# Layer 0 of a four-layer graph network: the transposed adjacency by turning bytes on chip instead of a second load, with an earlier first load and a first product across six PSUM banks

## The chip, the core and the metric

The kernel runs on one core of a Trainium2 chip, as one launch. Its inputs lie in the chip's memory, and the host only lays them out (it also writes a transposed copy of the adjacency, `adjt`). The metric is the device time of one execution in microseconds (us); the time before is the median of three runs.

A core has five engines that run side by side, each with its own queue of instructions in a fixed order: TensorE (PE, matrix products; PEld is its loading of the stationary operand), VectorE (DVE), ScalarE (ACT), GpSimd (POOL) and SyncE (SP, which here only issues transfers). Sixteen DMA engines move data between the memory and the core's SBUF. Products land in PSUM, which has eight banks of 2 KiB per partition; one partition is one of 128 rows.

## The reference

There are 16 samples of 1024 nodes with 128 features, and an adjacency `adj` of 1024 x 1024 int32 per sample, zeros and ones. Four graph layers follow each other, each with a residual and a layer norm; layers 1 to 3 are attention layers and are not touched here. Layer 0, cut to what matters:

```python
adjT = transpose(adj.astype(float32), (0, 2, 1))
w = masked_row_softmax(adjT)          # adj is 0/1: every neighbour gets 1/count
region = matmul(w, features)
region = batch_norm(matmul(region, kernel_1) + bias_1)
people = matmul(transpose(w, (0, 2, 1)), region)
people = batch_norm(matmul(people, kernel_2) + bias_2)
x = layernorm(x + people)
```

The batch norms take their means and squares over all samples, so all 16 samples must pass both products with the adjacency before layer 0 has an output.

## The kernel before

`fast_path` holds everything (a slower general path runs only where a flag says that `adj` was not of zeros and ones, which ACT finds out by summing squares). Layer 0 is the block from L657 to L799. It uses that the products with the small kernels commute with those over the graph: per sample it makes `zr`, the sum of the neighbours' features with a count; `zf`, `zr` over the count; `zw`, `zf` over the count again; and `yf`, the sum of `zw` over the transposed adjacency. What the batch norms need is gathered over all samples as two Gram matrices (`gram`, L674), of `zf` and of `yf`, each summed in a PSUM bank of its own. `yf` is stored to the memory as `people`, from where the later layers read it.

The products run in bf16 with float32 sums. `split3` (L721) cuts a float32 tile into three bf16 parts, whose sum is the value: ACT casts, DVE subtracts, ACT casts the rest, DVE subtracts again. The parts stand side by side as 3 x 130 = 390 columns, in `xs` (of x; the column behind the first part is one, and gives the count) and `zs` (of `zw`). The adjacency is the stationary operand: an int32 of zero or one, whose lowest byte is read as an 8-bit float with a stride of four bytes.

`product` (L737) runs over eight chunks c of 128 nodes. For each it takes one of six PSUM banks (`f_pz`), makes eight matmuls of 390 columns (L744), and lets DVE add the three parts in one reduce from 387 to 129 columns (L747), which frees the bank.

`region(b)` (L757) loads the sample's `adj` as four tiles of 1 MiB (`f_at`, six slots; `load_adj`, L729), loads and splits x of the next sample (`features`), has ACT do the eight sums of squares (L765), multiplies, and has DVE do the count, its reciprocal, `zf` (L774), `zw` (L775) and the split of `zw`. `spread(b)` (L779) loads the sample's `adjt` as four more tiles of 1 MiB (`f_att`, six slots), multiplies with `zs`, stores `yf` on ACT's queue (L786) and adds to a Gram matrix. The loop (L793) calls region of sample b and then spread of sample b − 1, so that PE has a product to make while DVE and ACT prepare the next moving operand:

```python
for b in range(B + 1):
    now = region(b) if b < B else None
    if yf is not None:
        gram(1, yf, b - 2)
    yf = spread(b - 1, *held) if b else None
    held = now
```

Each engine's order in layer 0 is set by the framework's scheduler from this program; where a buffer has slots, a load waits until the last reader of its slot is done. In front of the loop, six small loads of the weights stand first in SP's queue (L576 to L587), and PE makes a few products of weights alone (L637 to L647: three transposes into one bank, copies by ACT, three narrow products into another). They are used by `first_norm` in the last sample and in the layers behind. After layer 0, a short stretch computes the second batch norm, and layers 1 to 3 run from a plan with a fixed order that is written out in the file; it reads `adjt` itself and is not touched.

## Time and profile before

| | |
|---|---|
| median of three runs | 1693.37 us (1692.27 to 1694.13) |
| the profiled execution's own time | 1691.56 us |
| its span (first to last instruction) | 1689.7 us |
| mean granted clock of TensorE | 0.981 |
| layer 0, to its last product | 0 to 421.4 us |
| PE busy over the span | 1608.6 us (95%) |
| DVE, ACT, POOL busy | 1306.2 (77%), 1122.9 (66%), 361.2 us (21%) |
| read from the memory, written | 377.89 MB, 16.91 MB |

Some conventions of the views below. A row of the stage windows gives a stretch in us, its length, the busy time of PE, PEld, DVE, ACT and POOL with the number of instructions, the clock granted to TensorE, the mean busy share of the 16 DMA engines, and GB/s. A row of groups gives line, engine and operation, the output and inputs by name with their shapes, how many, then busy us and mean ns of one, then the engine's idle time ahead of them and what ended it. A row of a timeline gives the start in us, the duration, the engine and the instructions (x9: nine in a row), and in brackets the wait ahead of it and what ended it. SPq is SP's queue, where a DMA is issued. Matmuls are pipelined: the mean of one contains overlap with its neighbours.

The stretch around 240 to 265 us serves as the steady sample: one passage of the loop, with region of one sample and spread of the one before. Over layer 0 the period of the loop is 25.27 us.

### The profile page before, as it was taken

The numbers are of one execution on the slowest core, as the hardware profiler recorded it, in microseconds if no ns is written. First come the engines' busy times: TensorE is split into PE (matmuls) and PEld (weight loads), VectorE is DVE, ScalarE is ACT, GpSimd is POOL, SyncE is SP. The second block draws the span as 40 slices with busy tenths as digits, with TensorE's granted clock in tenths as the row PEclk, the third lists the DMA queues.
The fourth block names the chain that finished last, engine by engine and source line by source line (L and its number), as shares of the span: only waits on it lengthen the run. The fifth ranks groups of instructions, "written<-read, shape, count | busy, mean of one in ns | idle before, by whom it ended". The sixth has DMA issues, their size and how long they took to land. (4 is left out here: it accounts for less than half of the span.)

```text
span 1689.7 us, 34809 instructions
## 1 busy us (share of the span) xinstructions
PE 1608.6 (95%) x13007; PEld 1443.5 (85%) x13023; DVE 1306.2 (77%) x2924; ACT 1122.9 (66%) x2911; POOL 361.2 (21%) x615
## 2 busy tenths in 40 slices
PE   6999999999569999999999999999999999999996
PEld 4666666666468999999999999999999999999996
DVE  4565565565367889898988989898898989898775
ACT  6555555552446777778677777877777787777575
POOL 0000000000121232323233132422323241331221
PEclk9999999999579999999999999999999999999999
DMA  8999999997355667667766666777666676766652
GB/s 319 382 365 393 362 372 392 352 388 280 115 184 175 200 183 213 201 203 215 214 205 200 205 196 210 215 210 206 210 194 194 217 210 205 211 189 195 187 158 77
DMA packets 395155, 397.16 MB, mean 235 GB/s; under 512 B 11104, under 2 KB 339680, under 8 KB 394976
## 3 DMA queue, kind: packets, MB, share of 16 engines
q1 hardware_dynamic: 378336, 386.45, 70.3%
q10 hardware_dynamic: 16640, 8.39, 1.7%
q8 instruction: 104, 1.70, 0.4%
q14 instruction: 75, 0.61, 0.1%
HBM read 377.89 MB, written 16.91 MB: 234 GB/s over the span
## 5 line engine op out<-in xcount | busy, mean ns | idle before, releaser
L1191 PE MATMUL f_pbank<-f_rows,f_p 128*128 128x129 f32 x4096 | 495.6, 275 | 0.8 <-DVE f_p L1178 0.8
L1191 PEld LDWEIGHTS f_pbank<-f_rows,f_p 128*128 128x128 f32 x4096 | 475.2, 191 | 3.6 <-DVE f_q L1045 2.6
L1141 PE MATMUL f_pbig<-f_xt,f_hw 128*128 128x128 f32 x2304 | 303.1, 276 | 3.9 <-ACT f_xt L977 1.5
L1141 PEld LDWEIGHTS f_pbig<-f_xt,f_hw 128*128 128x128 f32 x2304 | 279.0, 192 | 7.2 <-ACT f_xt L977 1.8
L1170 DVE TENSOR_TENSOR f_q<-f_q,f_e 128x1024 f32<-128x1024 f32 (+7 forms) x256 | 193.5, 756 | 117.1 <-ACT f_q L1163 88.8
L1163 ACT ACTIVATE f_q<-f_pbig,f_neg_shift 128x1024 f32<-128x1024 f32 (+7 forms) x256 | 189.3, 739 | 140.7 <-PE f_pbig L1155 139.2
L1091 PE MATMUL f_pbig<-f_q,f_p 128*128 128x128 f32 x2048 | 254.4, 278 | 5.7 <-ACT f_q L1085 5.7
L1091 PEld LDWEIGHTS f_pbig<-f_q,f_p 128*128 128x128 f32 x2048 | 242.7, 194 | 7.1 <-ACT f_q L1085 7.1
L1167 ACT ACTIVATE f_e<-f_pbig,f_neg_shift 128x1024 f32<-128x1024 f32 (+7 forms) x256 | 188.4, 736 | 37.2 <-PE f_pbig L1155 32.0
L1178 DVE TENSOR_TENSOR f_p<-f_q,f_a 128x1024 f32<-128x1024 f32 (+7 forms) x256 | 192.5, 752 | 1.9
L744 PE MATMUL f_pz<-f_zs,f_att 128*128 128x390 bf16 x1024 | 181.0, 328 | 3.1 <-DVE f_yf L747 2.9
L744 PE MATMUL f_pz<-f_xs,f_at 128*128 128x390 bf16 x1024 | 178.9, 330 | 4.9 <-DVE f_xs L727 4.2
L765 ACT ACTIVATE f_junk<-f_at,f_sq_bias 128x1024 bf16<-128x1024 int32 x128 | 146.9, 1148 | 51.4 <-DVE f_yf L747 47.9
L1076 DVE SCALAR_TENSOR_TENSOR f_p<-f_u,f_r,f_u 128x1024 f32<-128x1024 f32 x128 | 163.3, 1276 | 6.4 <-DMA f_u<-f_u_dram 6.4
L744 PEld LDWEIGHTS <-f_at 128*128 128x128 fp8e4 x1024 | 100.1, 98 | 73.0 <-issue 6.1
L744 PEld LDWEIGHTS <-f_att 128*128 128x128 fp8e4 x1024 | 100.1, 98 | 69.6 <-issue 6.5
L1079 DVE SCALAR_TENSOR_TENSOR f_p<-f_p,f_a 128x1024 f32<-128x1024 f32 x128 | 156.3, 1221 | 2.3
L1182 DVE TENSOR_TENSOR f_p<-f_pbig,f_a 128x128 f32<-128x128 f32 (+6 forms) x224 | 152.4, 680 | 0.1
L747 DVE TENSOR_REDUCE f_zr<-f_pz 128x129 f32<-128x387 f32 x128 | 63.2, 552 | 111.8 <-PE f_pz L744 111.7
L952 POOL TENSOR_SCALAR f_ln_var<-f_sq 128x1 f32<-128x1 f32 (+2 forms) x96 | 38.5, 401 | 500.3 <-ACT f_junk L941 500.3
L1155 PE MATMUL f_pbig<-f_ident,f_q 128*128 128x128 f32 x896 | 135.1, 273 | 4.1 <-DVE f_q L1170 3.4
L914 ACT ACTIVATE f_junk<-f_rows,f_total 128x128 f32<-128x128 f32 x256 | 102.7, 401 | 15.2 <-DVE f_rows L1015 5.1
(160 smaller groups left out, 2121.5 us busy)
## 6 DMA issues: line engine op xcount, KB each, us to landing
f_a<-in_adjt_dram SPq DMA_DIRECT2D x384, 512.0 KB, 4.5
f_at<-in_adj_dram SPq DMA_DIRECT2D x64, 1024.0 KB, 9.3
f_att<-in_adjt_dram SPq DMA_DIRECT2D x64, 1024.0 KB, 13.7
f_u<-f_u_dram SPq DMA_DIRECT2D x32, 512.0 KB, 5.8
f_xn<-in_x_dram SPq DMA_DIRECT2D x16, 512.0 KB, 11.2
f_people<-f_yf ACTq DMA_DIRECT2D x16, 512.0 KB, 16.9
f_yn<-f_people SPq DMA_DIRECT2D x16, 512.0 KB, 3.8
f_x<-in_x_dram SPq DMA_DIRECT2D x16, 512.0 KB, 4.4
```

Source lines behind the costliest of these rows:

```text
L744: nc.tensor.matmul(pz[:, :3 * K], a8[:, j % 2, c * 512:(c + 1) * 512:4], moving[:, j].rearrange("p k d -> p (k d)"), start=(j == 0), stop= ...
L765: nc.scalar.activation(junk, at[c // 2][:, c % 2, :], AF.Square, bias=sq_bias, accum_out=squares[:, b, c:c + 1])
L1076: p = op(DVE, 1.2, lambda e, t, t2, *_, j=j: nc.vector.scalar_tensor_tensor(e, t2, ln.r[:, j:j + 1], t, ALU.mult, ALU.max), [key("r", j)], ...
L1079: op(DVE, 1.24, lambda t, e, j=j: nc.vector.scalar_tensor_tensor(e, e, 1.0, t.rearrange("p c n -> p (c n)"), ALU.mult, ALU.mult, accum_out ...
L1091: nc.tensor.matmul(t[:, c * D:(c + 1) * D], q[:, c * P:(c + 1) * P], hn[:, j, :], start=False, stop=(j == C - 1 and c % 4 == 3))
L1141: nc.tensor.matmul(t[:, j * P:(j + 1) * P], hw[:, j * P:(j + 1) * P], xt[:, mine], start=True, stop=True)
L1163: nc.scalar.activation(q[:, blocks, :], t[:, c * P:].rearrange("p (c n) -> p c n", n=P), AF.Exp, bias=neg_shift)
L1167: nc.scalar.activation(e[:, c * P:], t[:, c * P:], AF.Exp, bias=neg_shift, scale=SLOPE)
L1170: nc.vector.tensor_max(q[:, blocks, :], q[:, blocks, :], e[:, c * P:].rearrange("p (c n) -> p c n", n=P))
L1178: nc.vector.tensor_mul(t[:, c * P:].rearrange("p (c n) -> p c n", n=P), q[:, blocks, :], k[:, c:, :])
L1182: nc.vector.tensor_mul(t[:, :c * P].rearrange("p (c n) -> p c n", n=P), s[:, :c * P].rearrange("p (c n) -> p c n", n=P), k[:, :c, :])
L1191: nc.tensor.matmul(t[:, :D + 1], w[:, j * P:(j + 1) * P], xl[:, j, :], start=(j == 0), stop=(j == C - 1))
```

## The change

Only layer 0 and what stands in front of it change.

- The loads of x and adj of sample 0 are issued first, then the six weight loads (`load_weights`). The products of weights become `of_weights`, called in passage b = 1 between region and spread, with PSUM banks of the `f_pz` class.
- `load(b + 1)` issues x and all four tiles of adj of the next sample at the start of a passage; `f_at` has eight slots, two samples.
- `adjt` is no longer loaded in layer 0. `pack` copies the int32 of adj to bytes, eight copies of 128 x 1024 a sample, odd chunks on DVE and even ones on ACT, in an order that puts the two bytes of a pair side by side. `turned` reads the bytes as 16-bit elements and turns them by eight transposing transfers of 128 x 512 elements (128 KiB) on SP's queue. The second product reads the turned bytes with a stride of two.
- `xs` and `zs` are dense: 385 and 387 columns. The count column of the first product stands behind the three parts; DVE's reduce is 384 to 128 columns, and ACT copies the count column of each bank.
- x of sample 0 is split in four pieces of two chunks. The first product of sample 0 runs over six banks at once, tile by tile of adj; its last two chunks and all other products go bank by bank.

```diff
-        xss.append(l0c.tile([P, C, 3, K], BF16, name=f"f_xs{i}"))
+        xss.append(l0c.tile([P, C, 3 * D + 1], BF16, name=f"f_xs{i}"))
+            nc.gpsimd.memset(xss[i][:, :, 3 * D:], 1.0)
-        zss.append(l0c.tile([P, C, 3, K], BF16, name=f"f_zs{i}"))
+        zss.append(l0c.tile([P, C, 3 * (D + 1)], BF16, name=f"f_zs{i}"))
...
+        def pack(tiles):
+            packed = l0.tile([P, C, N], U8, name="f_packed")
+            for c in range(C):
+                src = tiles[c // 2][:, c % 2, :].rearrange("p (q k h) -> p q k h", q=C // 2, k=2)
+                dst = packed[:, c, :].rearrange("p (q h k) -> p q k h", q=C // 2, k=2)
+                if c % 2:
+                    nc.vector.tensor_copy(dst, src)
+                else:
+                    nc.scalar.copy(dst, src)
+            return packed
+
+        def turned(packed):
+            t = l0.tile([P, C // 2, N], BF16, name="f_turned")
+            for c in range(C):
+                nc.sync.dma_start_transpose(t[:, :, c * P:(c + 1) * P], packed[:, c, :].bitcast(BF16))
+            return t.bitcast(F8)
+
+        def by_columns(tiles):
+            return lambda j, c: tiles[j // 2].bitcast(F8)[:, j % 2, c * 512:(c + 1) * 512:4]
+
+        def by_rows(t8):
+            return lambda j, c: t8[:, j // 2, c * 2 * P + j % 2:(c + 1) * 2 * P:2]
...
+            def multiply(pz, j, c):
+                nc.tensor.matmul(pz[:, :wide], block(j, c), moving[:, j], start=(j == 0), stop=(j == C - 1))
+
+            def gather(pz, c):
+                nc.vector.tensor_reduce(dst[:, c, :n], pz[:, :3 * n].rearrange("p (k d) -> p d k", k=3),
+                                        AX.X, ALU.add)
+                if wide > 3 * n:
+                    nc.scalar.copy(dst[:, c, n:n + 1], pz[:, 3 * n:wide])
+
+            pzs = [l0p.tile([P, 512], F32, name="f_pz") for _ in range(across)]
+            for j in range(C):
+                for c in range(across):
+                    multiply(pzs[c], j, c)
...
-            product(zr, at, xs)
+            packed = pack(at)
+            product(zr, by_columns(at), xs, D, across=0 if b else 6)
...
-            tiles = load_adj(adjt, b, "f_att")
-            product(yf, tiles, zs, first_norm() if b == B - 1 else ())
+            product(yf, by_rows(a8), zs, D + 1, first_norm() if b == B - 1 else ())
...
-        features(0)
-        held, yf = None, None
+        held, yf, new = None, None, load(0)
+        load_weights()
+        for c in range(0, C, 2):
+            split3(xss[0][:, c:c + 2], new[0][:, c:c + 2], D)
         for b in range(B + 1):
-            now = region(b) if b < B else None
+            coming = load(b + 1) if b + 1 < B else None
+            now = region(b, new[1], coming) if b < B else None
+            new = coming
+            if b == 1:
+                of_weights(lambda: l0p.tile([P, 512], F32, name="f_pz"))
```

## The prediction

> **What bounds the kernel now.** I read the stage windows first (us; PE, PEld, DVE, ACT, POOL busy with counts; granted clock; DMA share; GB/s).
>
> ```profile
> 0.00:14.80 14.80, 2.56 (x9) 1.84 (x10) 3.33 (x10) 6.37 (x11) 1.81 (x19) 1.00 0.77 275
> 14.80:39.60 24.80, 23.56 (x134) 13.59 (x135) 14.44 (x21) 22.12 (x34) 0.00 (x0) 1.00 0.92 336
> 39.60:421.40 381.80, 378.71 (x2432) 248.62 (x2430) 229.27 (x373) 196.95 (x283) 3.79 (x17) 1.00 0.97 366
> 421.40:520.00 98.60, 64.41 (x377) 55.45 (x378) 52.71 (x145) 42.01 (x130) 18.86 (x39) 0.71 0.41 139
> ```
>
> Only layer 0, the first 421.4 us, is touched. PE is busy 378.7 of its steady 381.8 us; DVE 60%, ACT 52%. The DMA share of 0.97 looks like a second bound, but PE hardly waits for a load: the transfers fill whatever time the slots allow. So the 64 MiB of loads that go are worth little themselves. Next, the groups of one steady sample (window 240.24 to 265.5).
>
> ```profile
> L744 PE MATMUL f_pz<-f_xs,f_at 128*128 128x390 bf16 x66 | 11.6, 328 | 0.0
> L744 PE MATMUL f_pz<-f_zs,f_att 128*128 128x390 bf16 x64 | 11.3, 328 | 0.2 <-DVE f_yf L747 0.2
> L765 ACT ACTIVATE f_junk<-f_at,f_sq_bias 128x1024 bf16<-128x1024 int32 x8 | 9.2, 1148 | 3.6 <-DVE f_yf L747 3.3
> L747 DVE TENSOR_REDUCE f_zr<-f_pz 128x129 f32<-128x387 f32 x9 | 4.5, 550 | 7.3 <-PE f_pz L744 7.3
> L724 ACT CAST f_xs<-f_xn 128x1024 bf16<-128x1024 f32 x2 | 2.1, 1031 | 0.0
> ```
>
> A mean of 328 ns counts overlap. The PE timeline gives the pitch, and the one stall of a sample:
>
> ```profile
> 251.03 1.66 PE L744 MATMUL f_pz<-f_zs,f_att 128*128 128x390 bf16 x9
> 252.93 0.83 PE L744 MATMUL f_pz<-f_zs,f_att 128*128 128x390 bf16 x4 [0.24 <-DVE f_yf L747]
> ```
>
> (1.66 − 0.33)/8 = 166 ns a matmul; the gram's 16 take 1.95 us, 112 ns each. A sample is 128 × 0.166 + 32 × 0.111 = 24.8 us against a period of 25.27. The rest, 0.40 us, is this stall: PE has filled six banks while DVE stands in the chain from counts to the split of zs, shown by DVE's timeline:
>
> ```profile
> 245.14 1.23 DVE L774 TENSOR_TENSOR f_zf<-f_zr,f_zw 128x1024 f32<-128x1024 f32 x1
> 246.40 1.23 DVE L775 TENSOR_TENSOR f_zw<-f_zf,f_zw 128x1024 f32<-128x1024 f32 x1
> 251.17 1.24 DVE L727 TENSOR_TENSOR f_zs<-f_rest,f_zs 128x1032 bf16<-128x1032 f32 x1 [1.13 <-ACT f_zs L726]
> 252.32 1.95 DVE L747 TENSOR_REDUCE f_yf<-f_pz 128x129 f32<-128x387 f32 x4
> ```
>
> The waits have it in 13 samples. Last, the start:
>
> ```profile
> 3.58 0.43 SPq L754 DMA_DIRECT2D f_xn<-in_x_dram  x1
> 4.06 2.26 SPq L733 DMA_DIRECT2D f_at<-in_adj_dram  x4
> 13.45 1.23 DVE L727 TENSOR_TENSOR f_xs<-f_rest,f_xs 128x1024 bf16<-128x1024 f32 x1 [1.75 <-ACT f_xs L726]
> 14.82 12.09 PE L744 MATMUL f_pz<-f_xs,f_at 128*128 128x390 bf16 x64 [3.69 <-DVE f_xs L727]
> ```
>
> x lands at 8.13, the four tiles of adj at 10.68, 13.24, 15.79, 18.43 (2.55 us a MiB); the product waits for the split of x.
>
> **The change, part by part.**
>
> Columns. 1024 first products go from 390 to 385 columns, 1024 second ones from 390 to 387: by 166 ns in proportion, 2.1 and 1.3 ns, together −3.4 us. Neither end is far: PE is the bound throughout.
>
> The stall. In the new order DVE takes the reduces of yf between the steps of the split, so PE's banks come free sooner: 13 × 0.40 = −5.2 us, if nothing is late in its place. That is the question, since DVE and ACT get more. Per sample each gets four packs (1024 int32 to bytes). No row shows one. Nearest on ACT are the cast (1.03) and the square (1.15), on DVE the 1024-wide subtraction (1.23): I take 1.05 and 1.2, the nearest rows. The lower end is the shortest cast, 0.93; above I allow a byte write with stride half as much again, 1.8, since no row writes bytes or works through four dimensions. ACT also gets eight copies of one count column (0.16 us for such a copy at L719): 13.9 + 4.2 + 1.3 ≈ 19.5 us of work. DVE: 15.2 + 4.8 = 20 us. Both lie beside PE's 24.5 us; but a loop runs through both. From the last count copy, DVE does cnt, zf, zw, the two subtractions, eight reduces of yf, its packs and eight of zr, of which about 16.7 us must follow one another; then ACT's rest of the sample, eight copies, two packs, two squares and a cast (1.3 + 2.1 + 2.3 + 1.0 = 6.7); some 0.4 for handing over. 23.8 us: 0.8 below PE's period. Six packs lie in this loop, so it binds PE when they average over 1.35 us, and the period is back at 25.27 when they average 1.45. Past that each further 0.1 us per pack is 0.6 us × 15 = 9 us. The first pack of a sample also waits until the transposes of two samples earlier have read their buffer; behind it on DVE are reduces that free PE's banks. With transposes as priced next they are done half a period before.
>
> Transposes against loads. Per sample SP drops four loads of adjt and issues eight transposing transfers of 128 KiB. Issues: an issue on SP takes 0.43 us, so 8 × 0.43 replaces 4 × 0.57, SP having 13 issues in 24.6 us: free. If SP were held for all of a small transfer (1.62 us, below), it would be 8 × 1.62 + 5 × 0.5 = 15.5 us, still under the period. In SP's order the transposes of a sample stand behind the loads of the next (eight slots), 11.5 us of transfer, and have PE's whole first product of that sample to land in. The engines: 4.5 MiB at 2.55 = 11.5 us, plus the store of people (0.5 MiB, 1.3 us), 12.8 us, leaving 11.8 us, or 1.47 us a transpose. No transpose is in the trace. Below: as bytes at the load's rate, 0.32 us. Above: pieces of 32 bytes at 10 ns (packets of 4 and 80 bytes took 9 and 11), 256 per engine: 2.6 us. I take pieces of 256 bytes, for what one transfer writes on a partition is four runs of 128 two-byte elements: 512 runs, 32 per engine, at 18 ns (between 11 at 80 bytes and 27 at 512), 0.6 us. DMA then has 12.8 + 4.8 = 17.6 of 24.6 us and stays hidden.
>
> Here the skill pulls both ways. The Trainium skill, "Advanced Engine Details and Errata", section X-Bar Transpose (TRN2), has transposes as fast as regular transfers, 350 to 400 GB/s, an estimate of 0.35 us each; its table in DGE: Hardware vs Software, though, calls hardware transposes the worse kind, and the DMA page ("DMA: Bandwidth & Descriptors", Latency and other measured facts) puts about 2 us on every transfer. One after another that would be 16 us, over the 11.8 us, and some +63 us; this trace's smallest load, 10 KB of vectors, took 1.62 us from issue to landing, but loads overlap. No run here shows a transpose.
>
> The start. Six weight loads move behind x and adj: x's issue stood at 3.58, and goes to 0.72, so all lands 2.86 earlier, the first tile at 7.8. The six weight issues (2.9 us) now stand between sample 0's adj and sample 1's x, which landed at 20.2 and is not wanted before 22. The weights' own users come at sample 1 and later. The first product runs across six banks as tiles come, to about 17.6. Its banks come free only by count copies, behind which ACT's order puts seven squares and four packs: 7.8 + 0.6 (rest of the quarter casts) + 7 × 1.15 + 4 × 1.05 + 0.2 = 20.9. Two banks of 8 × 0.164 end at 23.5. The split of sample 1 follows: ACT a square, four copies and a cast (to 23.7), DVE, ACT, DVE 1.2 + 1.05 + 1.2: region 1 begins at about 27, as before (14.82 + 12.09 = 26.9). Its eight banks again wait for copies behind six squares, four packs and two casts (some 12 us, to 39), and it ends near 42. Then the weight products, moved here, stand on PE: 1.5 us and a wait for ACT's copy of their transposes, 0.5 to 2. The second product of sample 0 starts at about 44 against 39.6: +4.4 us. Ends: −7.6 if only the tiles bind, +8 if the packs are dear or the transposes late (at 1 us each the eight of sample 0 stand before x of sample 2).
>
> Sum: −3.4 − 5.2 + 4.4 = −4.2 on the profiled execution's own 1691.56 us: 1687.4. That execution lies 1.8 under the median of the runs, so about 1689. Nothing past 421.4 changes but by shift; the clock's dip to 0.71 there moves along.
>
> **Rivals.** Transposes bind (ends slower). Place: the transfers of the steady samples; price 8 × (t − 1.47) × 15, at t = 2 us +63 us, at 2.6 +135; it decides from about 1.5 us a transpose. For it: the DMA share is 0.97 already, and small packets are dear. Against: the bytes of a sample, the store included, fall from 9 to 6 MiB. Chance 0.12.
>
> Packs bind (ends slower). Place: the loop through DVE and ACT; at 1.6 us a pack 0.15 × 6 × 15 = 13.5, with the start +18 us, at 1.8 +36; decides from 1.45. For it: the slack is only 0.8 us. Against: the output type has cost nothing so far (the subtraction takes 1.23 with f32 and bf16 out). Chance 0.22.
>
> Nothing to measure: the stall stays, in another place (ACT's count copies hold the banks), and columns and start cancel: 1693. Chance 0.06.
>
> The start goes as the tiles alone would let it, −7.6 instead of +4.4: 1677. For it: loads do land 2.9 earlier. Against: ACT's order. Chance 0.05.
>
> The forecast as worked out: 0.55.
>
> **How the numbers follow.** About 0.2% (3.4 us) is what a measurement of this kernel can tell from no change. The forecast's own spread, the start from 0 to +8 and the stall from gone to half left, is 1684 to 1697: of its 0.55 I put 0.38 below 1690, 0.15 within and 0.02 above. Faster is then 0.38 + 0.05 = 0.43; the same 0.15 + 0.06 + 0.03 (packs just at their limit) = 0.24; slower 0.02 + 0.12 + 0.19 = 0.33. The range leaves out the better start (0.05), transposes past 1.65 us (0.09) and packs past 1.65 (0.06), 0.20 in all: 1682 to 1716.
>
> **What the profile after would show.** Right: period 24.5 to 24.7, no wait of PE for yf, packs of 1.0 to 1.3 us, transposes under 1.4 us of queue time, DMA share near 0.7, the second product of sample 0 at 42 to 46. Wrong: a wait of every sample for f_turned (transposes), for f_pz by ACT's count copy or for zs (packs), or a start under 35 (better).

## The result: 8.6 us slower, and the profile after

The kernel after takes 1700.97 us (median of five runs, 1700.44 to 1705.13), the one before, run beside it, 1692.39 us (1690.89 to 1694.13). The ratio is 1.0056, with a 95% interval of 1.0041 to 1.0070: slower by 8.6 us. That is inside the range of 1682 to 1716, but on the other side of the forecast of 1689. The profiled execution after took 1703.0 us, with a span of 1701.2 us and a mean granted clock of 0.979, so it lies 2 us above the median of its runs.

Layer 0 holds the loss. The last matmul of its second products starts at 429.4 us against 421.1 before, 8.3 us later. What follows is shifted by that, give or take 1 to 2 us in the start of the attention layers; in this one execution the stretch after the last product of layer 3 also took 1.9 us longer, which the median doesn't show.

The stage windows of after, with the columns as before (length, busy time of PE, PEld, DVE, ACT and POOL with counts, granted clock, DMA share, GB/s):

```profile
0.00:7.95 7.95, 0.00 (x0) 0.00 (x1) 2.49 (x11) 3.26 (x8) 1.55 (x15) 1.00 0.74 266
7.95:42.76 34.81, 28.92 (x154) 16.84 (x154) 22.83 (x38) 32.80 (x65) 0.00 (x0) 0.95 1.09 311
42.76:140.06 97.30, 89.21 (x547) 57.10 (x547) 65.50 (x102) 73.76 (x127) 1.36 (x3) 0.96 0.98 295
140.06:400.89 260.83, 260.83 (x1682) 170.65 (x1680) 187.87 (x296) 174.29 (x322) 6.07 (x11) 1.00 0.80 230
400.89:429.70 28.81, 28.81 (x198) 20.29 (x196) 14.05 (x29) 2.54 (x4) 1.10 (x3) 1.00 0.06 19
```

From 140 us on PE is busy in all 260.83 us: the stall of each sample is gone. Samples 2 to 5, from 42.76 to 140.06 us, are the odd row: PE idles for 8.1 of 97.3 us and the granted clock is 0.96.

The PE timeline of a steady sample (start, duration, instructions) shows a period of 24.86 us (the next first product starts at 264.29), against 25.27 before, in which the pieces follow each other without a gap:

```profile
239.43 10.78 PE L772 MATMUL f_pz<-f_xs,f_at 128*128 128x385 bf16 x64
250.04 1.95 PE L678 MATMUL f_pgram<-f_yf 128*128 128x130 f32 x16
251.83 10.83 PE L772 MATMUL f_pz<-f_zs,f_turned 128*128 128x387 bf16 x64
262.50 1.95 PE L678 MATMUL f_pgram<-f_zf 128*128 128x130 f32 x16
```

The groups of that sample by shape (busy us and mean ns of one) give the packs' price, 1.04 us on ACT and 0.69 us on DVE:

```profile
L749 ACT CAST f_packed<-f_at 128x1024 uint8<-128x1024 int32 x5 | 5.2, 1040 | 0.0
L747 DVE CAST f_packed<-f_at 128x1024 uint8<-128x1024 int32 x4 | 2.6, 690 | 0.2 <-issue 0.2
```

The PE timeline of samples 2 to 5 shows where the loss sits. In brackets stand the wait and what ended it:

```profile
64.80 4.39 PE L772 MATMUL f_pz<-f_xs,f_at 128*128 128x385 bf16 x16 [3.27 <-ACT f_zr L778]
...
131.14 1.49 PE L772 MATMUL f_pz<-f_zs,f_turned 128*128 128x387 bf16 x8 [0.93 <-DVE f_yf L775]
135.28 1.77 PE L772 MATMUL f_pz<-f_zs,f_turned 128*128 128x387 bf16 x8 [2.65 <-DVE f_yf L775]
136.85 3.37 PE L678 MATMUL f_pgram<-f_zf 128*128 128x130 f32 x16
```

The stops are few, and two of them cost twice. Sixteen matmuls take 4.39 us at 64.8 where 16 × 0.166 would be 2.7, and the gram at 136.85 takes 3.37 us where the steady one takes 1.95. The windows of these stretches have the reason in the granted clock, 0.50:

```profile
64.80:67.90 3.10, 3.10 (x10) 1.46 (x10) 2.51 (x5) 3.10 (x9) 0.00 (x0) 0.50 1.02 407
136.50:139.70 3.20, 3.20 (x16) 3.17 (x15) 3.00 (x4) 3.20 (x5) 0.00 (x0) 0.50 1.02 403
```

What ACT had waited for before it freed the bank at 64.8 is in ACT's own timeline:

```profile
56.49 0.19 ACT L807 ACTIVATION_READ_ACCUMULATOR f_junk<-f_at,f_sq_bias 128x1 f32 x1
62.52 1.05 ACT L727 CAST f_xs<-f_xn 128x1024 bf16<-128x1024 f32 x1 [5.84 <-DMA f_xn<-in_x_dram]
63.47 1.14 ACT L807 ACTIVATE f_junk<-f_at,f_sq_bias 128x1024 bf16<-128x1024 int32 x1
...
64.61 0.20 ACT L778 COPY f_zr<-f_pz 128x1 f32<-128x1 f32 x2
```

ACT stands 5.84 us for x of sample 3. The count copies of L778, which free PE's banks, are queued behind that cast, so PE stops. And x is late because of SP's queue, whose timeline reads:

```profile
18.41 17.19 SPq L756 DMA_TRANSPOSE f_turned<-f_packed  x8
35.65 0.57 SPq L797 DMA_DIRECT2D f_xn<-in_x_dram  x1
36.32 2.07 SPq L736 DMA_DIRECT2D f_at<-in_adj_dram  x4
38.48 19.80 SPq L756 DMA_TRANSPOSE f_turned<-f_packed  x8
58.33 0.57 SPq L797 DMA_DIRECT2D f_xn<-in_x_dram  x1
...
188.15 11.35 SPq L756 DMA_TRANSPOSE f_turned<-f_packed  x8
```

An ordinary load holds SP for about half a microsecond. Eight transposes hold it for 17.2 and 19.8 us in the first samples and for 11.4 us in steady ones. The holds are not waits for packs: the last packs of samples 0 to 4 end at 19.4, 36.7, 55.7, 77.6 and 95.8 us, each before the second transpose of its sample is issued (20.1, 41.5, 64.5, 84.8 and 107.8). The loads of the next sample stand behind them: x(2) is issued at 35.65 us, x(3) only at 58.33, the next at 79.10, 100.69 and 122.22. A round of 21 to 23 us is shorter than PE's 24.9, so the lag is worked off, but slowly: it lasts until sample 6.

Waits of 42.76 to 140.06 us (total us, times, longest) give the sum:

```profile
ACT f_xs L727 <- DMA f_xn<-in_x_dram: 15.1, 4, 5.8
...
ACT f_junk L807 <- DMA f_at<-in_adj_dram: 7.9, 2, 6.3
PE f_pz L772 <- DVE f_yf L775: 4.5, 3, 2.6
PE f_pz L772 <- ACT f_zr L778: 3.6, 2, 3.3
```

The long wait for adj, 6.3 us, has one more cause in the queue: between x(6) at 122.2 and adj(6) at 124.9 stand x(7) and two early loads for the layers behind, 0.5 MiB each.

The start, in the PE timeline:

```profile
20.60 2.81 PE L772 MATMUL f_pz<-f_xs,f_at 128*128 128x385 bf16 x16 [1.91 <-ACT f_zr L778]
26.71 9.75 PE L772 MATMUL f_pz<-f_xs,f_at 128*128 128x385 bf16 x48 [3.30 <-DVE f_cnt L812]
...
42.76 10.82 PE L772 MATMUL f_pz<-f_zs,f_turned 128*128 128x387 bf16 x64
```

The first product begins at 7.95 instead of 14.82 us, and its last two banks wait for ACT's count copies until 20.6, as forecast (20.9). The second product of sample 0 starts at 42.76 against 39.64, when 16 matmuls of the gram are done instead of 6.

The account of PE up to the last matmul of the second products, from the distances between starts of matmuls: a stop is what exceeds the steady distance by more than 0.23 us, half pace what exceeds it by 0.085 to 0.23 us.

| us | before | after |
|---|---|---|
| first product starts | 14.8 | 8.0 |
| half pace until 45 us | 1.2 | 4.2 |
| stops until 45 us | 1.8 | 6.5 |
| weight products, moved in | – | 1.0 |
| stops after 45 us | 5.3 | 8.9 |
| half pace after 45 us | 0.0 | 3.1 |
| sum | 23.1 | 31.7 |

That is +8.6, less 0.8 for the narrower columns, +7.8 us of the 8.3 measured.

Behind the stops the half pace is the granted clock, as the windows show. At the very start it is not: the first matmuls of layer 0 stand 0.32 us apart from 7.95 to 13.4 us (2.6 of the 4.2 us), where the profile's rows show a granted clock of 1.00. Why is open.

### The profile page after: what moved, and what is told of

It is laid out like the page before. It is cut to its first block, busy times and chain, and to the rows that moved or that the text cites. A ratio compares the mean times of both kernels' runs of the same rounds, so it can differ in the third digit from the quotient of the medians.

```text
span 1701.2 us, 35177 instructions
## 1 busy us (share of the span) xinstructions
PE 1610.3 (95%) x13007; PEld 1443.5 (85%) x13023; DVE 1352.0 (79%) x2994; ACT 1183.9 (70%) x3109; POOL 369.1 (22%) x611
## 5 line engine op out<-in xcount | busy, mean ns | idle before, releaser
L772 PE MATMUL f_pz<-f_xs,f_at 128*128 128x385 bf16 x1024 | 178.9, 335 | 18.0 <-DMA f_at<-in_adj_dram 8.0
L772 PEld LDWEIGHTS <-f_at 128*128 128x128 fp8e4 x1024 | 102.4, 100 | 90.2 <-issue 17.9
L772 PE MATMUL f_pz<-f_zs,f_turned 128*128 128x387 bf16 x1024 | 174.4, 329 | 3.6 <-DVE f_yf L775 3.6
L772 PEld LDWEIGHTS <-f_turned 128*128 128x128 fp8e4 x1024 | 100.4, 98 | 71.6 <-issue 4.0
L775 DVE TENSOR_REDUCE f_zr<-f_pz 128x128 f32<-128x384 f32 x128 | 68.9, 554 | 58.5 <-PE f_pz L772 58.0
L982 ACT ACTIVATE f_rows<-f_rows,f_off,f_rstd 128x128 f32<-128x128 f32 x256 | 110.9, 486 | 3.4 <-POOL f_off L978 3.2
```

Of the source, the lines that this page charges most:

```text
L772: nc.tensor.matmul(pz[:, :wide], block(j, c), moving[:, j], start=(j == 0), stop=(j == C - 1))
```

## The experiments

The theory after the result: the transposes hold SP's queue, so the loads behind them start late, and ACT, which takes its work in order, stands for x and adj with the bank-freeing copies behind it. Three rivals stood against it: the transposes load the DMA engines themselves (the first rival of the prediction); ACT's new work, packs and count copies, delays PE (the second); loads and transposes slow each other down whatever queue they are in. The start was a question of its own. Each ratio below is to the kernel before, run beside it, whose median was 1691.5 to 1691.8 us.

### x from another queue

```diff
-            nc.sync.dma_start(xn, x[b].rearrange("(c p) d -> p c d", p=P))
+            (nc.gpsimd if b else nc.sync).dma_start(xn, x[b].rearrange("(c p) d -> p c d", p=P))
```

> The loads of x from sample 1 on go from SP's queue to POOL's, nothing else. Theory SP: eight transposes hold SP's queue for 17 to 20 us, the issue of the next x stands behind them, ACT waits for x (5.8, 2.6, 3.4 and 3.3 us in the changed kernel) with the count copies and the casts of zs behind it in its order, and PE stops at 61, 111, 117 and 130 to 140 us, with half clock behind the longer stops, 12 us in all. Then these waits go, the last product of layer 0 ends near 419 to 422 us instead of 429.7, and the time is 1690 to 1694 us. Theory ACT: ACT simply has too much work in the first samples (32.8 of 34.8 us busy between 8 and 43 us), wherever x comes from. Then the stops stay, in other places, and the time is 1699 to 1701.

Measured: 1705.97 us, 1.0083 [1.0066, 1.0099]. The wait for x went as the theory has it, from 15.1 to 2.8 us, but the time rose by 5 us, which no theory expected. A queue without transposes runs ahead: x(1) and x(2) were issued at 1.9 and 7.9 us and travelled beside adj of sample 0, whose second tile landed at 12.4 instead of 10.5 us. Adj was late in place of x, PE stopped for 2.4 to 3.4 us at four places, and the last matmul of the second products began at 431.8. So this is no cure, and the run gives no verdict on the cause.

### All packs on DVE

```diff
-                if c % 2:
-                    nc.vector.tensor_copy(dst, src)
-                else:
-                    nc.scalar.copy(dst, src)
+                nc.vector.tensor_copy(dst, src)
```

> All eight packs of a sample on DVE (0.69 us each in the trace, against 1.03 on ACT), so that ACT has 4.1 us a sample less and DVE 2.8 more. Theory ACT: the stops at 18.4, 23.1 and 37.3 us (2.1, 3.5, 0.5, and 1.5 at half clock) shrink by more than half, the later ones too, 1690 to 1694. Theory SP: the start gains 3 to 5 us, the waits for x remain as they are, 1695 to 1698.

Measured: 1700.07 us, 1.0051 [1.0034, 1.0067]. Four packs of 1.04 us leave ACT in every sample, and the time is that of the changed kernel within what can be told. ACT only waits longer: 26.7 us for x in the first 140 us, against 17.9, and PE stops for 2.3 us before 62 and 2.7 us before 134 us. So its packs are not what makes ACT late.

### The count column back in DVE's reduce

```diff
-            xss.append(l0c.tile([P, C, 3 * D + 1], BF16, name=f"f_xs{i}"))
-            nc.gpsimd.memset(xss[i][:, :, 3 * D:], 1.0)
+            xss.append(l0c.tile([P, C, 3 * (D + 1)], BF16, name=f"f_xs{i}"))
+            for part in range(3):
+                edge = part * (D + 1) + D
+                nc.gpsimd.memset(xss[i][:, :, edge:edge + 1], 0.0 if part else 1.0)
...
-            product(zr, by_columns(at), xs, D, across=0 if b else 6)
+            product(zr, by_columns(at), xs, D + 1, across=0 if b else 6)
```

> The count stays in the three parts as before (387 columns in both products, one reduce from 387 to 129), and ACT copies no count. PE's banks then come free by DVE alone. Both theories: PE's stops that end with a count copy (18.4, 61.2 and 116.9 us: 2.1, 3.4 with 1.5 at half clock, 0.5) go; 387 columns instead of 385 cost 1024 x 0.8 ns, 0.9 us. Theory ACT: what ACT is spared (1.3 us a sample) helps the rest too, 1691 to 1694. Theory SP: ACT still waits for x with zs behind it, so the stop at 130 to 140 stays, 1695 to 1697.

Measured: 1701.22 us, 1.0052 [1.0035, 1.0069]. No copy by ACT frees a bank any more, and the time stays. The stops move to other places; PE's timeline of this kernel has the first at once, where the scheduler put the gram of sample 0 ahead of the first product of sample 1 and PE must wait for `zf`:

```profile
14.79 5.15 PE L774 MATMUL f_pz<-f_xs,f_at 128*128 128x387 bf16 x29
25.16 1.64 PE L680 MATMUL f_pgram<-f_zf 128*128 128x130 f32 x6 [5.22 <-DVE f_zf L819]
```

The count copies are the door through which late loads reach PE, not the cause: with that door shut the time comes in by DVE's `yf` and `zf`.

### adjt loaded again, all else as changed

```diff
-            packed = pack(at)
...
-            return zf, zs, turned(packed)
+            return zf, zs, None
...
-            product(yf, by_rows(a8), zs, D + 1, first_norm() if b == B - 1 else ())
+            att = []
+            for q in range(0, C, 2):
+                t = l0.tile([P, 2, N], I32, name="f_att", bufs=4)
+                nc.sync.dma_start(t, adjt[b, q * P:(q + 2) * P, :].rearrange("(c p) n -> p c n", p=P))
+                att.append(t)
+            product(yf, by_columns(att), zs, D + 1, first_norm() if b == B - 1 else ())
```

> The changed kernel with adjt loaded again (four tiles a sample, four slots) and without packs and transposes; the earlier first loads, the six banks, the dense columns, the count copies and the moved weight products stay. If the turn (packs, transposes, and what they hold up) is what costs, under either theory, the first samples run without the waits for x, the period stays at 24.9 us, and the time falls to 1687 to 1691. Rival: the start and the moved weight products cost by themselves, then it is 1692 to 1696; and if the loads of 9 MiB a sample bind (23 of 24.9 us by 2.55 us a MiB), the period is back at 25.3 or more, and it is above 1695.

Measured: 1693.16 us, 1.0008 [0.9998, 1.0018]. Without the turning (packs and transposes) the loss is gone; the turning costs 7.8 us more than loading adjt in this way. The window that was the odd row has a busy PE here, at a DMA share of 1.04 and 399 GB/s:

```profile
42.76:140.06 97.30, 97.30 (x613) 63.29 (x614) 60.56 (x92) 62.04 (x117) 0.77 (x4) 0.98 1.04 399
```

The period is 24.81 us. So in this stretch four more loads of 1 MiB a sample cost PE nothing, and eight transposes of a quarter of those bytes do. It doesn't follow that the rest of the change is worth nothing, since this kernel pays elsewhere: by the account above its weight products take 2.6 us longer than in the changed kernel, and at 406 to 416 us, with four slots for adjt, its stops add up to 3.3 us. Its waits of PE (total us, times, longest) have these under adjt:

```profile
PE f_pz L772 <- DMA f_att<-in_adjt_dram: 2.8, 3, 2.1
```

### All loads from sample 2 on from another queue

```diff
-                nc.sync.dma_start(t, adj[b, q * P:(q + 2) * P, :].rearrange("(c p) n -> p c n", p=P))
+                (nc.gpsimd if b > 1 else nc.sync).dma_start(
+                    t, adj[b, q * P:(q + 2) * P, :].rearrange("(c p) n -> p c n", p=P))
...
-            nc.sync.dma_start(xn, x[b].rearrange("(c p) d -> p c d", p=P))
+            (nc.gpsimd if b > 1 else nc.sync).dma_start(xn, x[b].rearrange("(c p) d -> p c d", p=P))
```

> All loads of x and adj from sample 2 on go to POOL's queue; SP keeps samples 0 and 1, the weights and the transposes. Moving x alone made adj late in its place, so the theory is now wider. Theory SP: loads and transposes share one queue, a transpose issued behind loads holds it until the loads have gone through, and the next sample's loads wait for eight of these, so that each of the first samples gets its adj only some 21 us after the one before, starting late. With the loads in a queue of their own adj of sample 2 starts near 27 us instead of 36, ACT's waits for adj and x after 43 us (43 and 15 us) fall by more than half, the stops of PE after 60 us (3.4, 1.0, 0.5, 1.1, 2.8 us and 4.5 of half clock) fall under 4 us together, layer 0's last product is at 419 to 423 us instead of 429.4, and the time 1690 to 1694 us. Rival, the engines: packs, count copies and squares are too much for ACT in the first samples whatever the loads do; then the stops stay and it is 1698 to 1702. Rival, the DMA engines: transposes and loads now mix and slow each other down; then transposes take over 6 us to land, the second products wait for f_turned, above 1702.

Measured: 1716.74 us, 1.0142 [1.0117, 1.0168]. ACT's waits for loads fell as the theory expected (2.8 us for x, 1.1 for adj in 140 us), and the time rose by 16 us: this is what the third rival had foreseen. Freed of SP's queue, the loads filled the DMA engines ahead of the transposes, of which the eight of sample 0 landed 16 to 27 us after their issue. PE's timeline shows them late in their own name, and the last stop goes back to them too, since a pack of DVE waited 30.3 us for the transposes to read its buffer:

```profile
49.15 1.50 PE L773 MATMUL f_pz<-f_zs,f_turned 128*128 128x387 bf16 x8 [2.45 <-DMA f_turned<-f_packed]
54.10 2.25 PE L773 MATMUL f_pz<-f_zs,f_turned 128*128 128x387 bf16 x8 [3.45 <-DMA f_turned<-f_packed]
73.31 8.03 PE L773 MATMUL f_pz<-f_zs,f_turned 128*128 128x387 bf16 x32 [16.95 <-ACT f_zr L779]
```

SP's queue thus did not only delay the loads; it also kept them from crowding out the transposes. This run doesn't yet say whether the transposes' bytes or their number cost the time.

### Only the loads a sample ahead, on the kernel before

```diff
-        def load_adj(src, b, name):
+        def load_adj(src, b, name, bufs):
...
-        def region(b):
-            at = load_adj(adj, b, "f_at")
+        def region(b, at, coming):
...
         for b in range(B + 1):
-            now = region(b) if b < B else None
+            coming = load(b + 1) if b + 1 < B else None
+            now = region(b, new[1], coming) if b < B else None
+            new = coming
```

> The kernel before with one edit: x and all four tiles of adj of the next sample are issued at the start of a passage, with eight slots for adj and four for adjt instead of six and six. No dense columns, no turn, the start as before. In the order of DVE both subtractions of the split of x then stand behind the reduces of yf. If it is this order that takes away the stall of 0.40 us a sample (and neither the turn nor the columns), the period is 24.85 us instead of 25.27, and the time 1686 to 1689 us. Rival: four slots for adjt make its tiles late; then PE waits for f_att, and the time is 1692 or more.

Measured: 1697.79 us, 1.0033 [1.0022, 1.0044]. The period is 24.91 us with 390 columns and both loads: the stall of 0.40 us a sample is gone by the order alone, in which the subtractions for `xs` come later than the reduces of `yf`. But it is slower. At the start the new order puts the gram of sample 1 ahead of the second product of sample 0, and PE waits there for `zf`; with the half pace around it the start costs 6.8 us by the account, more than the 5.3 us that the stall gave:

```profile
45.28 3.81 PE L676 MATMUL f_pgram<-f_zf 128*128 128x130 f32 x16 [3.87 <-DVE f_zf L773]
48.88 11.83 PE L744 MATMUL f_pz<-f_zs,f_att 128*128 128x390 bf16 x64
```

The rest is the rival named beforehand: with four slots the last tiles of adjt are late, and between 397 and 422 us PE's stops add up to 4.2 us. PE's waits of layer 0 (total us, times, longest):

```profile
PE f_pz L744 <- DMA f_att<-in_adjt_dram: 3.5, 4, 1.8
```

### Weights first again

```diff
-        held, yf, new = None, None, load(0)
         load_weights()
+        of_weights(lambda: l0p.tile([P, 512], F32, name="f_pz"))
+        held, yf, new = None, None, load(0)
...
-            if b == 1:
-                of_weights(lambda: l0p.tile([P, 512], F32, name="f_pz"))
```

> The changed kernel with the weight loads and the weight products back in front of x and adj. The first product starts 2.9 us later (10.8 us), but PE has not the 1.8 us of weight products, nor the 0.5 us wait for their copies, between the first product of sample 1 and the second of sample 0. If the turn's queue is what decides the first samples, everything shifts by 0 to 3 us: 1700 to 1704. If the moved weight products were the loss, 1695 to 1698.

Measured: 1702.12 us, 1.0060 [1.0043, 1.0077]: about 1 us above the changed kernel, not to be told from it. The first product starts at 11.3 instead of 8.0 us and the second product of sample 0 at 47.5 instead of 42.8, but the stops after 45 us add up to 6.8 us instead of 8.9, and the last matmul of the second products starts only 2.0 us later (431.4). So the moved weight products are not the loss.

### The first product bank by bank

```diff
-            product(zr, by_columns(at), xs, D, across=0 if b else 6)
+            product(zr, by_columns(at), xs, D, across=0)
```

> The changed kernel with the first product of sample 0 bank by bank, as all others are. It can finish its first bank only when the last tile of adj has landed (15.7 us), so it ends near 27 us instead of 23.3, but each count copy is wanted later. If the tile-by-tile start is worth what it saves, 2 to 4 us slower than the changed kernel, 1703 to 1706. If ACT's order behind it decides (first product of sample 1 at 27 us in either case), no change, 1700 to 1702.

Measured: 1701.08 us, 1.0056 [1.0039, 1.0073]. But this edit didn't do what it was meant to. PE's timeline shows that it doesn't go bank by bank:

```profile
7.42 1.79 PE L772 MATMUL f_pz<-f_xs,f_at 128*128 128x385 bf16 x5 [7.42 <-DMA f_at<-in_adj_dram]
9.98 9.29 PE L772 MATMUL f_pz<-f_xs,f_at 128*128 128x385 bf16 x43 [0.77 <-DMA f_at<-in_adj_dram]
```

A bank can take two matmuls from each tile of adj, so the five made before the second tile landed went to three banks at least, and 48 were done by 19.3 us; bank by bank the first would have been done only behind the last tile, at 15 us. The scheduler put the six banks side by side on its own, and the last matmul of the first product starts at 22.6 us against 23.1 in the changed kernel. So what the six banks are worth stays untested. What the run does show is that the first product of sample 1 (26.2 us against 26.7) begins when x(1) is split, behind ACT's squares and packs, and not when tiles land.

### Half of the transposes

```diff
+        half = [l0c.tile([P, C // 2, N], BF16, name=f"f_turned{i}") for i in range(2)]
+        for t in half:
+            nc.gpsimd.memset(t, 0.0)
-        def turned(packed):
-            t = l0.tile([P, C // 2, N], BF16, name="f_turned")
-            for c in range(C):
+        def turned(packed, b):
+            t = half[b % 2]
+            for c in range(0, C, 2):
```

> The changed kernel with four of the eight transposes of a sample (those of the odd chunks are left out, and their columns of the turned tile stay zero, so the second product leaves out half its rows). Nothing else is changed. Theory, as it now stands: in the first samples the loads of a sample, then the eight transposes behind them at 1.3 to 1.6 us each, then the next loads follow one another on SP's queue, about 21 us a round, and start late; the load ahead and the transposes want the DMA engines in the same stretch. With four transposes a round is 5 us shorter and the transposes of sample 0 take 6 us less: adj of sample 2 is issued near 30 us instead of 36, the waits of ACT for x and adj after 43 us fall from 58 us to under 25, the stops of PE after 60 us from 8.9 (with 3 to 4 of half clock) to under 4, and the time is 1689 to 1694 us. Rival, ACT's packs and count copies are what is too much: they are all still there, the stops stay, 1699 to 1702.

Measured: 1689.44 us, 0.9986 [0.9977, 0.9995]. This kernel leaves out half the rows of the second product (it multiplies zeros there). All packs, squares, copies and matmuls are still done, and PE has no stop between 45 and 400 us. SP's queue:

```profile
17.20 11.03 SPq L760 DMA_TRANSPOSE f_turned<-f_packed  x4
28.32 0.53 SPq L801 DMA_DIRECT2D f_xn<-in_x_dram  x1
```

x(2) is issued 7.3 us earlier than at 35.65. This clears ACT's new work: the transposes are the cause. Whether by their number or by their bytes this run can't say, since both were halved.

### Transposes twice as large, half as many

```diff
-            t = l0.tile([P, C // 2, N], BF16, name="f_turned")
-            for c in range(C):
-                nc.sync.dma_start_transpose(t[:, :, c * P:(c + 1) * P], packed[:, c, :].bitcast(BF16))
+            t = l0.tile([P, C, C // 2, P], BF16, name="f_turned")
+            for c in range(0, C, 2):
+                nc.sync.dma_start_transpose(
+                    t[:, c:c + 2].rearrange("p c q n -> p (c q) n"),
+                    packed[:, c:c + 2, :].rearrange("p c n -> p (c n)").bitcast(BF16))
...
-            return lambda j, c: t8[:, j // 2, c * 2 * P + j % 2:(c + 1) * 2 * P:2]
+            return lambda j, c: t8[:, c, j // 2, j % 2:2 * P:2]
```

> The changed kernel with four transposes a sample of 128 x 1024 elements (two chunks each) in place of eight of 128 x 512; the turned tile is laid out by row chunk so that each writes one run per partition. Same bytes, half the instructions. With half the transposes left out the stops of the first samples went; this tells whether it was their bytes or their number. If each transpose holds SP for a time of its own (1.31 us in the steady samples, whatever it moves), four hold it 5 to 6 us a sample instead of 11 to 12, x of sample 2 is issued near 29 us instead of 35.7, the stops after 60 us go, the last product of layer 0 is at 418 to 422 us and the time 1688 to 1692. If the hold goes by the bytes, two of the new ones take as long as two pairs of the old, 2.6 us, nothing changes but the layout, and the time is 1699 to 1702.

Measured: 1689.18 us, 0.9985 [0.9976, 0.9994], 11.8 us below the changed kernel with the same bytes turned. So the bytes alone are not the cause. First the line of the transposes in the changed kernel, with durations on SP in ns (minimum, median, maximum):

```profile
L756 SPq DMA_TRANSPOSE f_turned<-f_packed x128: 1188/1266/6599, 18.4 to 396.7; - x128
```

The same line, SP's queue and the window of samples 2 to 5 in this kernel:

```profile
L756 SPq DMA_TRANSPOSE f_turned<-f_packed x64: 1232/1759/9143, 18.1 to 380.8; - x64
...
18.12 14.81 SPq L756 DMA_TRANSPOSE f_turned<-f_packed  x4
32.98 0.57 SPq L799 DMA_DIRECT2D f_xn<-in_x_dram  x1
...
35.85 15.27 SPq L756 DMA_TRANSPOSE f_turned<-f_packed  x4
51.18 0.57 SPq L799 DMA_DIRECT2D f_xn<-in_x_dram  x1
...
42.76:140.06 97.30, 97.30 (x624) 62.86 (x625) 75.02 (x120) 84.78 (x150) 2.88 (x4) 1.00 1.07 310
```

A transpose of 256 KiB can hold SP for as little as 1.23 us, one of 128 KiB for 1.19, though the median grows from 1.27 to 1.76; a steady sample's sum falls from about 11.4 us to between 7.1 and 7.7. In the first two samples, behind loads, it falls less, from 17.2 and 19.8 us to about 15, and x(2) went out at 32.98 where some 29 was expected: a miss in size. But x(3) goes out 7.2 us earlier, ACT's wait for x falls from 15.1 to 2.8 us, and PE is busy throughout.

On the DMA engines the two kernels are alike. Where transposes land close behind each other, they are 0.4 to 0.5 us apart at 128 KiB and 0.8 to 1.0 at 256 KiB, so the engines' time goes by the bytes; and the DMA share of samples 2 to 5 is even higher here, 1.07 against 0.98, with PE busy. So it is not the load on the engines that stopped PE; what is left is how long the queue is held. One thing is not told apart: the layout of the turned tile changed with the number, and it may have a part in the shorter hold.

### The same, with all packs on DVE

> As the one with paired transposes, and all packs on DVE (0.69 us each, against 1.03 on ACT), which leaves ACT 4 us a sample and puts the count copies of the first product right behind their reduces. If the hold goes by the number of transposes, the first samples have no stop after 60 us, and the start gains the 2 us that packs on DVE gave by themselves: last product of layer 0 at 415 to 419 us, 1684 to 1689 us, faster than both kernels. If it goes by bytes, about as packs on DVE alone: 1698 to 1701.

Both edits together measured 1687.21 us, 0.9971 [0.9962, 0.9980]: the fastest kernel here, 4.4 us below the one before and 13.8 below the changed one. By the medians ACT's packs now count for about 2 us, but the two intervals overlap, and the profiled execution, the slowest of its runs at 1690.36 us, doesn't show the gain: its last matmul of the second products starts at 419.3 us, against 417.4 with the packs on both engines. One stop of 1.8 us remains at 124 us, where none was expected.

### The split of x on POOL, on the kernel before

```diff
-        def split3(dst, src, n):
+        def split3(dst, src, n, engine=nc.vector):
...
-            split3(xss[b % 2], xn, D)
+            split3(xss[b % 2], xn, D, nc.gpsimd if b > 1 else nc.vector)
```

> The kernel before with one edit: from sample 2 on, the two subtractions of the split of x are made by POOL, which has nothing to do in layer 0, instead of DVE. If the stall of 0.40 us a sample comes from DVE standing in its chain with those two subtractions (2.4 us) ahead of the count, it goes in 13 samples: period 24.85 us, 5.2 us less, 1686 to 1688 us. Rivals: POOL is so slow at it (over 8 us for the two) that ACT's second cast of x holds up the cast of zs behind it, then the stall grows, 1692 to 1700; or POOL takes DVE's reads of SBUF, then DVE's 1.23 us rows grow and nothing is gained, 1690 to 1693.

Measured: 1721.30 us, 1.0178 [1.0164, 1.0192], far above the 1686 to 1688 expected and above both rivals, 1692 to 1700 for a slow POOL and 1690 to 1693 for a POOL that slows DVE. This was the other way to take the split out of DVE's chain without touching the start. The timeline of the two engines:

```profile
260.70 2.06 POOL L727 TENSOR_TENSOR f_xs<-f_rest,f_xs 128x1024 bf16<-128x1024 f32 x1 [1.15 <-ACT f_xs L726]
...
260.85 3.00 DVE L774 TENSOR_TENSOR f_zf<-f_zr,f_zw 128x1024 f32<-128x1024 f32 x1
263.88 1.23 DVE L775 TENSOR_TENSOR f_zw<-f_zf,f_zw 128x1024 f32<-128x1024 f32 x1
```

DVE's `zf` takes 3.00 us beside POOL's subtraction, and `zw` just behind it, alone, the usual 1.23. So the second rival has the mechanism, at a far higher price than it gave: POOL needs 2.05 us for one subtraction, not over 4. PE's stall grew from 0.40 to 2.1 us a sample and the period to 27.06.

## Why the prediction was wrong, and where it was right

- **The stall**, −5.2 us: right. No stop of a steady sample is left, and DVE makes reduces of `yf` between the steps of the split (four of them from 254.2 to 258.9 us), as the step said. The run with loads ahead alone shows that the order does it, and neither the turning nor the columns. There the reduces of `yf` stand behind the split of `zs` as before (from 255.75 us on), and the subtractions for `xs` moved behind most of them, so the stall can go in another way than the step's.
- **The columns**, −3.4 us: mis-sized; −0.8 measured. The distance between matmuls is 166.6 ns at 390 columns, 166.7 at 387 and 165.8 at 385. "In proportion" failed: 387 columns saved nothing, and 385 saved 0.8 ns over 1024 matmuls. Why is open.
- **The start**, +4.4 us: the mechanism right, the size a little high. The product of sample 1 began at 26.7 (forecast 27), the second product of sample 0 at 42.76 (forecast 44). By the account the start cost about +1.9 us: more stops (+4.7), more matmuls at half pace (+3.0) and the moved weight products (+1.0), less 6.8 for the earlier first product.
- **Packs**: 1.04 us on ACT as forecast (1.05), 0.69 on DVE, well under 1.2. The rival of dear packs fell. Its limits were summed a little high: 24.6 − 23.8 us over six packs that average 1.15 gives 1.28 us, not 1.35, and 1.40, not 1.45, for the old period. The six measured 0.81 us on average, so nothing hung on it. With all packs on DVE the time stayed; with half the transposes and all packs the loss was gone.
- **Transposes on the DMA engines**: they landed 0.4 to 0.5 us apart where several were under way, below the forecast 0.6 and far from the 1.5 us from which the engines would bind. The first rival fell as it was priced, though the transposes were at fault. The page "DMA: Bandwidth & Descriptors" of the Trainium skill (Latency and other measured facts) gives transposes with a strided middle dimension 261 GB/s; by that 128 KiB would take 0.5 us, an estimate, and these runs agree; the 350 to 400 GB/s weighed in the prediction was not reached.
- **The step that failed** is "Issues": "If SP were held for all of a small transfer (1.62 us, below), it would be 8 × 1.62 + 5 × 0.5 = 15.5 us, still under the period", taken as free. In the steady samples the bound was good: SP is held 1.19 us at least and 1.27 in the median per transpose, 11.4 us a sample. With loads in flight it was not, since the eight transposes of each of the first five samples held SP for 16 to 20 us, where 8 × 1.62 is 13. And "under the period" doesn't make a term free: a queue that keeps up on average can still be late for what stands behind it. x(2) went out at 35.65, and the queue had only 2 to 4 us a round to make that good. The prediction had noted at the end of its start step that the transposes stand before x of sample 2, but only as a price if they were dear. The term put at nothing measured +12.0 us in samples 2 to 5: 8.9 of stops and 3.1 of half pace behind them.
- **The range and the signs.** That 1700.97 lies inside 1682 to 1716 is luck: the range was that wide for dear transposes and dear packs, and neither came. Of the signs of being wrong none appeared either, since they look for a wait in every sample, and the loss sits in the first six.

With the measured terms: −5.3 (stall) − 0.8 (columns) + 1.9 (start) + 12.0 = +7.8 us, against 8.3 measured at the end of layer 0 and 8.6 in the median.

Shown by the runs: that without the turning the loss is gone (adjt loaded again: 1.0008), that its packs are not the cause (half the transposes), and that fewer transposes on SP's queue take the loss away with the same bytes turned (pairs). Open: why a transpose holds SP, and longer behind loads; what part the new layout has in the pairs; what the six banks are worth; how much the start's remaining stops, 2 to 3.5 us each, could give; and part of the 1 to 2 us by which the attention layers' start shifts differently from the end of layer 0.

## What to carry to other kernels

Cost a moved or added transfer twice: by the time of the engines that move its bytes, and by the time for which its issue holds the queue; then ask which load stands behind it there, in the first samples as in the steady ones. An average under the period says that a lag is worked off, not that none arises. Where an instruction holds its queue, try fewer and larger ones, as the pairs did here. Giving the loads a queue of their own was worse in both runs that tried it, since they then ran ahead of what was needed first. And look in the trace whether the edit of an experiment reached the engine: a scheduler may undo it, as it did with the banks.

## What the runs showed of the hardware that was not expected

- A transposing transfer from SBUF to SBUF holds the issuing queue: 1.19 us at least for 128 x 512 elements of two bytes, 1.23 for 128 x 1024, where an ordinary load of 1 MiB takes about 0.5. Behind loads in flight one held it for up to 6.6 and 9.1 us, with all packs of its sample done before. Why, the trace doesn't show.
- Beside loads of another queue, transposes landed 16 to 27 us after their issue; alone they took 2.4 us.
- PE ran at a granted clock of 0.50 to 0.57 for about 3 us behind its stops of 3.30, 3.27 and 2.65 us in the changed kernel, and not behind that of 1.91. The length alone doesn't decide: a stop of 2.02 us was followed by a clock of 0.60 (first product bank by bank, 37.4 us), and one of 2.23 by the full clock (weights first, 88.1 us). The second half of such a stop's price is easily missed: 3.1 us after 45 us here.
- The first matmuls of layer 0 stand 0.32 us apart, twice the steady 0.166, in rows with a granted clock of 1.00 (10.5 to 13.5 us in the changed kernel).
- Two engines on 128 x 1024 float32 at once: POOL's subtraction took 2.05 us, and DVE's multiplication beside it 3.00 instead of 1.23.
